# First layer of a four-layer kernel: W products paired over two slots, convolution taps paired in odd slots, and four smaller moves

## The chip, the cores and the metric

The kernel runs on one core of a Trainium2 chip. The metric is the device time in microseconds of one execution. Engines are called PE (matrix engine), ACT (scalar engine), DVE (vector engine), POOL (GpSimd) and SP (the engine that issues most of the DMAs here).

## The reference

Four layers run one after the other on `x` of shape (4, 64, 64, 128), each as `x = x + layer(group_norm(x))`. Only the first layer is touched by the change; the other three (a Fourier layer, a spectral attention layer, a neighbourhood attention layer) stay as they are. The first layer is a two-dimensional selective scan. Cut to what is computed, for each of the 4 images:

```python
xz = gn(x) @ in_proj_w.T                 # 128 -> 512 channels
xh, z = split(xz, 2); z = silu(z)        # 256 channels each
xc = silu(depthwise_conv3x3(xh) + conv_b)
x0 = xc by rows, x1 = xc by columns      # (256, 4096)
xs = [x0, x1, reversed x0, reversed x1]  # 4 directions k
dts, B, C = split(x_proj_weight[k] @ xs[k], [8, 24])      # 8, 16, 16 rows
delta = softplus(dt_projs_weight[k] @ dts + dt_bias[k])   # (256, 4096)
# for each of 16 states n, along the 4096 positions:
h[n] = exp(delta * A[k, :, n]) * h[n] + delta * xs[k] * B[n]
y[k] = sum over n of h[n] * C[n], plus D * xs[k]
y = the four directions put back in place and added
out = (layer_norm(y) * z) @ out_proj_w.T
```

## The kernel before

**Units and slots.** `layer0` walks over 128 units: 4 images, 4 directions k, 8 pieces of 512 positions. A unit has 16 slots, one for each state n, so there are 2,048 slots. In the text, "slot 4" is the slot with n = 4 of some unit. The order in which instructions are written is the order on each engine (a manual schedule); the tile pools put in the waits.

**One slot.** POOL forms `dB` (L684: `du` times a row of B, 128x1024). For each of the two channel halves, ACT computes `dA` into a bank of PSUM (L689, three banks in rotation) and DVE runs the scan into `h` (L690). Then `transposed()` is called. It puts eight transposes of older states on PE (L538, into the single PSUM tile `pt`, two banks), then the W products of the tile transposed one slot before (L573: four matmuls of 32 columns each, `yT <- hT, W`, side by side in the array), and hands back a copy on ACT (L548, `hT <- pt`). "T" below is the eight transposes, "W products" the four matmuls. The transposes run 7 slots behind the scan (`LAG = 7`).

**The two `yT` banks.** The W products accumulate over the four groups of four states. For an earlier unit the last groups' products fall in slots 4 to 7 of the next one: the first of the two `yT` tiles is complete in slot 5, the second in slot 7. Each is then taken out (for the first direction of an image by a copy, L587, else by an add on DVE, L589), and the next unit starts to fill them in slot 8.

**The steps of the next unit.** A table gives them fixed places: in slot 6 on PE the small product `xd_ps` (L448, 48 rows), in slot 7 on ACT two copies out of it (`xd` L451 and `Ct` L456), in slots 7 and 9 on PE the two products `dp` (L465), from slot 8 to 12 the softplus (ACT L468 and L471, DVE L474) and `du` (POOL L477).

**Side work.** The input side of the next image and the output side of the previous one are generators. Each `yield` names a kind of piece, and after each slot at most one piece is put in, if `Side.due` says that the work is behind its pace (pieces done against slots gone by). A convolution has nine taps (L159, matmuls of 128x512 into one PSUM bank `cv`); one may start only in slot 11, and once it has started, `Side.inside` makes every following slot carry one tap, so it runs from slot 11 to slot 3 of the next unit. There are 52 such convolutions. They, and every other small product of the side work and of the steps, use one PSUM bank (`spare`, tag "m").

**Silu.** `silu` uses ACT three times (Exp, Ln, Exp; L631) and DVE once (L358). `later(place, ..., slots=...)` puts each in a given later slot: "act0" is behind the first `dA` of the slot, "act1" behind the second, "act2" behind the copy `hT`, "dve" ahead of the scans. After a convolution, that ends in slot 3, the Exp comes in slot 4 (act0), the Ln in slot 4 (act1), the second Exp in slot 5 (act0), the product on DVE in slot 6, and a copy by columns on ACT (`by_columns`, L369) in slot 7. The gates `z` are computed in the same way: a product `zp` (L177), Exp, Ln and Exp all in the slot after, the product on DVE in the slot after that.

Of the kernel before, what the change touches and what calls it, by code (L numbers as in the profile page):

```python
# [11 lines left out]
F32 = mybir.dt.float32  # L12
# [5 lines left out]
P = 128  # L18
# [64 lines left out]
def layer0(sh, A, x_in, x_out, scr, ahead):  # L83
# [7 lines left out]
    with ExitStack() as ctx:  # L91
# [60 lines left out]
        def conv(xn, s, bank):  # L152

            for t in range(9):
                yield "c"
                if t == 0:
                    pm = bank("cv")
                dy, dx = divmod(t, 3)
                nc.tensor.matmul(  # L159
                    pm,  # L160
                    lhsT=taps[:, s, t, :],
                    rhs=xn[:, dy : dy + 8, dx : dx + 64],
                    start=(t == 0),
                    stop=(t == 8),
                )
            return pm

        def grown(b, c, s, pm, later, e=None, gather=None):
            bias = conv_b[:, s : s + 1], conv_nb[:, s : s + 1]
            xo = silu(pm, *bias, scr(f"xr{b % 2}")[s, :, c * CH : (c + 1) * CH], later, (0, 1, 2), e)  # L170
            later("act0", gather or by_columns, xo, scr(f"xw{b % 2}")[s], c, slots=4)

        def gates(b, c, v, bank, later, es=(None, None)):
            for s in range(2):
                yield "z"
                zp = bank("zp")
                nc.tensor.matmul(zp, lhsT=w_in[:, 2 + s, :], rhs=v, start=True, stop=True)  # L177
                silu(zp, 0.0, 0.0, scr(f"z{b % 3}")[s, :, c * CH : (c + 1) * CH], later, (0, 0, 1), es[s])

        def rows():  # L180
            xn = tmp.tile([P, 10, 66], F32, name="xn", bufs=3)
# [170 lines left out]
        def silu(v, bias, minus, dst, later, wait, e=None):  # L352

            if e is None:
                e = tmp.tile([P, CH], F32, name="e", tag="t2", bufs=4)

            def product():
                nc.vector.scalar_tensor_tensor(e, v, bias, e, ALU.add, ALU.mult)  # L358
                nc.sync.dma_start(dst, e)

            later("act0", nc.scalar.activation, e, v, AF.Exp, scale=-1.0, bias=minus)
            later("act1", nc.scalar.activation, e, e, AF.Ln, bias=1.0, slots=1 + wait[0])
            later("act0" if wait[1] else "act2", nc.scalar.activation, e, e, AF.Exp, scale=-1.0, slots=1 + wait[1])
            later("dve", product, slots=1 + wait[2])
            return e

        def by_columns(xo, dst, c):
# [6 lines left out]
        def after(b, st, later, bands):  # L374

            for c in bands:
                yield "l"
                rows = slice(c * CH, (c + 1) * CH)
                if kept:
                    y = kept.pop()  # L380
                else:
                    y = tmp.tile([P, 4, 2 * P], F32, name="yf", tag="t4", bufs=4)
                    nc.sync.dma_start(y, tiles(scr(f"y2{b % 2}")[rows, :]))
                z = tmp.tile([P, 2, CH], F32, name="zf", tag="t4", bufs=4)
                nc.sync.dma_start(z, scr(f"z{b % 3}")[:, :, rows].rearrange("s p t -> p s t"))
# [12 lines left out]
                yg = tmp.tile([P, 2, CH], F32, name="yg", bufs=2)  # L398
                for s in range(2):
                    yield "m"  # L400
                    pt = spare("pg")
                    for q in range(4):
                        nc.tensor.transpose(pt[:, q * P : (q + 1) * P], y[:, q, s * P : (s + 1) * P], sh.ident)
                    norm = dict(scale=on_w[:, s : s + 1], bias=on_b[:, s : s + 1])
                    later("act0", nc.scalar.activation, yg[:, s, :], pt, AF.Identity, **norm)
                yield "f"
                xr = tmp.tile([P, 4, DM], F32, name="xr", tag="t2", bufs=4)
                nc.sync.dma_start(xr, tiles(x_in(b)[rows, :]))
                if b < NB - 1:
# [28 lines left out]
        def inputs(k, c, u, par, spare):  # L438
# [3 lines left out]
            du = tmp.tile([P, 2, CH], F32, name="du")  # L442
            bank = {}

            def project():
                bank["x"] = spare("xd_ps")[0:48, :]
                for s in range(2):
                    nc.tensor.matmul(bank["x"], lhsT=w_x[:, s, k, :], rhs=u[:, s, :], start=(s == 0), stop=(s == 1))  # L448

# [39 lines left out]
            return Bb  # L489

        spare = lambda name: psm.tile([P, CH], F32, name=name, tag="m")
        ring = [0]

        def any_bank(name):
# [25 lines left out]

        LAG = 7
        queue = []
        copied = None

        def transposed():

            nonlocal copied
            todo, copied = copied, None
            pt = None
            if queue:  # L530
                G = queue[0]
                q = G["q"]
                G["q"] += 1
                pt = ps.tile([P, 4, 2, P], F32, name="pt")
                for j in range(4):
                    t0 = q * P + j * 32
                    for s in range(2):
                        nc.tensor.transpose(  # L538
                            pt[:, j, s, :], G["h"][:, s, t0 : t0 + 32, :].rearrange("p t n -> p (t n)"), sh.ident
                        )  # L540
                if q == 3:
                    queue.pop(0)
            if todo is not None:
                products(*todo)
            if pt is not None:
                hT = tmp.tile([P, 4, 2 * P], F32, name="hT")
                copied = G, q, hT
                return lambda: nc.scalar.copy(hT, pt.rearrange("p j s d -> p j (s d)"))  # L548
            return lambda: None

# [78 lines left out]
        def later(place, f, *a, slots=1, **kw):  # L629

            todo.setdefault((slot + slots, place), []).append(lambda: f(*a, **kw))  # L631
# [10 lines left out]
        with tc.manual_schedule(engines=order):  # L642
            idle = lambda: None
            left = opening(any_bank, [idle, fetched, idle, begun, grown_steps, readied])
            u, ready, bd, Wd, Bb = (got[n] for n in ("u", "ready", "bd", "Wd", "Bb"))
            sides.append(Side(rest(left, spare, later), 18 * len(left), 0, 2 * NS * len(left)))
            for i, (b, k, c) in enumerate(units):
                if i % per == 0:
                    ln_st = small.tile([P, NJ, 1, 6], F32, name="ln_st")
                    first = len(left) if b == 0 else 0  # L650
                    if b + 1 < NB:
                        sides.insert(len(sides) if b == 0 else 0, Side(before(b + 1, spare, later), 17 + 8 * 22, NS * (i + first), (28 - first) * NS))
                rev = k >= 2
                pos = orders[b].index(k)
                pc = NCH - 1 - c if rev else c
# [16 lines left out]
                for n in range(NS):  # L672
# [14 lines left out]
                    for s in range(2):  # L687
# [4 lines left out]
                        )  # L692
                        steps(n, f"act{s}")
                        flush(f"act{s}")
                    copy = transposed() if slot >= LAG else (lambda: None)
                    copy()
                    steps(n, "act2")
                    flush("act2")
# [26 lines left out]

                    inside = [d for d in sides if d.inside]
                    free = not inside and slot >= taken
                    for d in inside or [d for d in sides if free and n in SIDE[d.need] and d.due(slot)][:1]:
                        taken = slot + SPACE[d.need]
                        d.free_at = slot + 1  # L730
                        d.step()
# [40 lines left out]
class Side:  # L772
# [7 lines left out]
    @property  # L780
    def inside(self):

        return self.need == "c" and self.run % 9 > 0

    def due(self, slot):
        wait = self.need == "l" and self.loads and slot < self.loads[0]
# [1404 lines left out]
```

## Time and profile before

| what | value |
|---|---|
| median of 3 runs | 7696.86 us (7693.64 to 7699.71) |
| the profiled execution, its time | 7694.64 us |
| its span, first to last instruction | 7692.9 us |
| mean granted clock of PE | 0.965 |
| first scan starts, last scan ends | 112.8 us, 5645.7 us |
| busy share of the span: PE, DVE, ACT, POOL | 82%, 88%, 79%, 74% |
| busy in 500 to 1500 us: PE, DVE, ACT, POOL | 85%, 98%, 95%, 93% |

The last row is from the busy times of that stretch alone: in the first layer four engines are nearly full at once, and the shares over the whole span mix this with the other three layers. A row of a group reads: line, engine, operation, output and inputs with their shapes, how often; then busy time in all and the mean of one; then the idle time of the engine just before these instructions, and what ended most of it. A row of the timeline reads: start, length, engine, line, operation, tiles, how many in a row, and in brackets the idle time before and what ended it. A matmul of 512 columns shows as two records, as does each W product (so a tap is "x2", and the four W products are "x8"); a transpose is one record.

### The profile page before, as it was taken

What the parts mean: (1) busy time and instruction counts of PE and PEld (TensorE: products, weight loads), DVE (VectorE), ACT (ScalarE), POOL (GpSimd) and SP (SyncE); (2) the same over time, 40 slices, a digit from 0 to 9 for tenths busy, and PEclk for the clock granted to TensorE, in tenths of its full rate; (3) what the DMA queues carried; (4) which work ended last, traced back from release to release, by engine and by line L of the source; (5) the groups of instructions that cost most, each with busy time, mean ns of one, the idle gap of its engine ahead of it and who ended that gap; (6) DMA issues with size and microseconds to landing.
All of it is one profiled execution on the core that took longest, in us unless ns stands there. A gap on an engine that the chain in (4) does not pass through costs nothing.

```text
span 7692.9 us, 140985 instructions
## 1 busy us (share of the span) xinstructions
PE 6324.7 (82%) x52796; PEld 3997.2 (52%) x52796; DVE 6751.7 (88%) x8113; ACT 6094.9 (79%) x9683; POOL 5694.2 (74%) x2718
## 2 busy tenths in 40 slices
PE   7888888888889877888887777787789978676789
PEld 3544444444455544445554444454467756564566
DVE  7999999999999999999999999999966655656678
ACT  7999999999999999999999999999843323314667
POOL 4999999999999999999999999999930024123233
PEclk8999999999999999999999999999999978788899
DMA  6555556555656655465565445555532241231332
GB/s 173 171 169 177 176 171 180 168 172 166 189 174 182 189 188 171 155 183 184 174 193 185 166 168 180 176 182 180 176 107 67 63 115 52 77 103 41 103 97 81
DMA packets 1325856, 1158.87 MB, mean 151 GB/s; under 512 B 694134, under 2 KB 1119698, under 8 KB 1258227
## 3 DMA queue, kind: packets, MB, share of 16 engines
q1 hardware_dynamic: 1320898, 1147.43, 48.7%
q8 instruction: 416, 6.82, 0.4%
q10 hardware_dynamic: 4272, 2.43, 0.1%
q14 instruction: 270, 2.20, 0.1%
HBM read 956.37 MB, written 189.21 MB: 149 GB/s over the span
## 4 chain that ended last, share of the span: by engine, by line
PE 34%; ACT 31%; DVE 19%; issue 8%; POOL 4%; DMA 2%; SPq 1%; ACTq 0%; DVEq 0%; POOLq 0%
ACT hT L548 12%; DVE h L690 12%; ACT dA L689 12%; PE pt L538 7%; PE cv L159 5%; PE yT L573 4%; POOL dB L684 3%; ACT e L631 2%; PE pf L917 2%; PE po L930 1%; ACT delta L468 1%; PE pt L1870 1%; PE pu L1161 1%; PE pa L1161 1%; PE pb L1161 1%
## 5 line engine op out<-in xcount | busy, mean ns | idle before, releaser
L690 DVE TENSOR_TENSOR_SCAN h<-dA,state,dB 128x512 f32<-128x512 f32 x4096 | 4921.4, 1268 | 127.0 <-POOL dB L684 48.0
L684 POOL TENSOR_TENSOR dB<-du,Bb 128x1024 f32<-128x1024 f32 x2048 | 4816.6, 2391 | 162.2 <-DVE h L690 121.9
L538 PE MATMUL pt<-ident,h 128*128 128x128 f32 x16384 | 2221.1, 279 | 824.8 <-ACT hT L548 809.6
L689 ACT ACTIVATE dA<-delta,A_neg 128x512 f32<-128x512 f32 x4096 | 2750.0, 695 | 118.3 <-DVE h L690 95.8
L538 PEld LDWEIGHTS pt<-ident,h 128*128 128x128 f32 x16384 | 1810.0, 142 | 1866.0 <-ACT hT L548 1642.5
L548 ACT COPY hT<-pt 128x1024 f32<-128x1024 f32 x2048 | 2077.2, 1014 | 178.6 <-PE pt L538 158.6
L573 PE MATMUL yT<-hT,W 128*32 128x256 f32 x16384 | 1380.2, 409 | 0.3
L573 PEld LDWEIGHTS yT<-hT,W 128*32 128x32 f32 x16384 | 455.8, 150 | 342.6 <-issue 330.2
L159 PE MATMUL cv<-xn,taps 128*128 128x512 f32 x936 | 526.9, 644 | 2.9 <-DVE delta L474 2.9
L1161 POOL TENSOR_TENSOR xg<-xg,so 128x1024 f32<-128x1024 f32 x16 | 39.3, 2467 | 620.0 <-PE pu L1161 619.4
L1908 POOL TENSOR_TENSOR S<-S,sm 128x784 f32<-128x784 f32 x128 | 191.4, 1495 | 414.6 <-DVE sm L1906 243.1
L477 POOL TENSOR_TENSOR du<-delta,u 128x512 f32<-128x512 f32 x256 | 329.2, 1286 | 188.7 <-DVE delta L474 172.3
L465 PE MATMUL dp<-xd,w_dt 65*128 65x512 f32 x512 | 288.7, 646 | 65.7 <-ACT Ct L456 43.8
L448 PE MATMUL xd_ps<-u,w_x 128*48 128x512 f32 x512 | 249.4, 610 | 18.8 <-DVE e L358 17.6
L1915 ACT ACTIVATE S<-S,mx 128x196 f32<-128x196 f32 x512 | 228.0, 449 | 32.2 <-DVE mx L1942 29.8
L159 PEld LDWEIGHTS cv<-xn,taps 128*128 128x128 f32 x936 | 139.2, 188 | 180.6 <-issue 163.2
L918 ACT ACTIVATE h<-pf,b 128x512 f32<-128x512 f32 x128 | 87.7, 687 | 118.8 <-PE pf L917 100.7
L474 DVE SCALAR_TENSOR_TENSOR delta<-delta,dp 128x512 f32<-128x512 f32 x256 | 171.2, 669 | 3.9 <-ACT delta L471 0.8
L1161 POOL TENSOR_TENSOR WX<-wr,Xs 128x544 f32<-128x544 f32 x40 | 60.7, 1517 | 152.2 <-issue 62.9
L1870 PE MATMUL pt<-ident,S 128*98 128x128 f32 x1024 | 166.3, 287 | 3.4 <-POOL S L1908 2.0
L1161 DVE TENSOR_TENSOR WX<-wr,Xs 128x544 f32<-128x544 f32 x88 | 74.1, 860 | 104.4 <-PE pz L1161 59.5
L465 PEld LDWEIGHTS dp<-xd,w_dt 65*128 65x128 f32 x512 | 76.5, 188 | 170.7 <-ACT Ct L456 97.4
(377 smaller groups left out, 7101.9 us busy)
## 6 DMA issues: line engine op xcount, KB each, us to landing
Bb<-l_B SPq DMA_DIRECT2D x512, 1024.0 KB
W<-l_W SPq DMA_DIRECT2D x512, 256.0 KB
l_y<-y SPq DMA_DIRECT2D x127, 512.0 KB
u<-l_xr SPq DMA_DIRECT2D x64, 512.0 KB
u<-l_xw SPq DMA_DIRECT2D x64, 512.0 KB
y<-l_y SPq DMA_DIRECT2D x56, 512.0 KB
V<-l_v SPq DMA_DIRECT2D x512, 49.0 KB
y<-l_y SPq DMA_DIRECT2D x80, 256.0 KB
```

The source lines that it names most:

```text
L159: nc.tensor.matmul(pm, lhsT=taps[:, s, t, :], rhs=xn[:, dy : dy + 8, dx : dx + 64], start=(t == 0), stop=(t == 8),)
L448: nc.tensor.matmul(bank["x"], lhsT=w_x[:, s, k, :], rhs=u[:, s, :], start=(s == 0), stop=(s == 1))
L465: nc.tensor.matmul(bank[s], lhsT=w_dt[:, k, s * P : (s + 1) * P], rhs=xd, start=True, stop=True)
L477: nc.gpsimd.tensor_tensor(du[:, s, :], delta[:, s, :], u[:, s, :], ALU.mult)
L538: nc.tensor.transpose(pt[:, j, s, :], G["h"][:, s, t0 : t0 + 32, :].rearrange("p t n -> p (t n)"), sh.ident)
L548: return lambda: nc.scalar.copy(hT, pt.rearrange("p j s d -> p j (s d)"))
L573: nc.tensor.matmul(U["yT"][e][32 * jo : 32 * jo + 32, qo % 2, :], lhsT=U["Ws"][G["g"]][:, :, 4 * q + j], rhs=hT[:, j, :], start=((e, jo) n ...
L684: nc.gpsimd.tensor_tensor(dB, du, B_now[:, q : q + 1, :].to_broadcast([P, 2, CH]), ALU.mult)
L689: nc.scalar.activation(dA, delta[:, s, :], AF.Exp, scale=A_neg[:, k, s, n : n + 1])
L690: nc.vector.tensor_tensor_scan(h[:, s, :, q], dA, dB[:, s, :], state[:, s, n : n + 1], ALU.mult, ALU.add)
L1161: r = f(*args, **kw)
L1870: nc.tensor.transpose(pt[:, half, hp, :], U["S"][:, e, hp, 98 * half : 98 * half + 98], sh.ident)
```

## The change

- **W products in pairs.** In slots 1, 3, 11, 13 and 15 `transposed` holds the W products back; the next slot puts in both, one group behind the other. For this `hT` has three buffers in place of two, and `yg` has one in place of two.
- **Taps in pairs.** `conv` yields at every second tap, and a convolution that has started goes on only in odd slots: two taps each in slots 11, 13, 15 and 1, one in slot 3. The counts that set the side work's pace follow (10 for 18, 14 for 22), and `inside` counts 5 pieces for 9.
- **`xd_ps` in a free `yT` bank.** In slot 6 it takes the `yT` tile that was complete in slot 5.
- **Silu spread.** After a convolution: Exp in slot 4, Ln in slot 5, Exp in slot 6 (all act0), product on DVE in slot 7. For `z` the new form gives the places that it had.
- **Column copy** in slot 13 in place of slot 7 (`slots=10`).

```diff
             for t in range(9):
-                yield "c"
+                if t % 2 == 0:
+                    yield "c"
...
         def grown(b, c, s, pm, later, e=None, gather=None):
-            xo = silu(pm, *bias, scr(f"xr{b % 2}")[s, :, c * CH : (c + 1) * CH], later, (0, 1, 2), e)
-            later("act0", gather or by_columns, xo, scr(f"xw{b % 2}")[s], c, slots=4)
+            xo = silu(pm, *bias, scr(f"xr{b % 2}")[s, :, c * CH : (c + 1) * CH], later, (("act0", 2), ("act0", 3), 4), e)
+            later("act0", gather or by_columns, xo, scr(f"xw{b % 2}")[s], c, slots=10)
...
-                silu(zp, ..., later, (0, 0, 1), es[s])
+                silu(zp, ..., later, (("act1", 1), ("act2", 1), 2), es[s])
...
-            later("act1", nc.scalar.activation, e, e, AF.Ln, bias=1.0, slots=1 + wait[0])
-            later("act0" if wait[1] else "act2", nc.scalar.activation, e, e, AF.Exp, scale=-1.0, slots=1 + wait[1])
-            later("dve", product, slots=1 + wait[2])
+            (log, a), (exp, b), c = wait
+            later(log, nc.scalar.activation, e, e, AF.Ln, bias=1.0, slots=a)
+            later(exp, nc.scalar.activation, e, e, AF.Exp, scale=-1.0, slots=b)
+            later("dve", product, slots=c)
...
-                yg = tmp.tile([P, 2, CH], F32, name="yg", bufs=2)
+                yg = tmp.tile([P, 2, CH], F32, name="yg", bufs=1)
...
+            outer = spare if spare is any_bank else free_bank
             def project():
-                bank["x"] = spare("xd_ps")[0:48, :]
+                bank["x"] = outer("xd_ps")[0:48, :]
...
+        free_bank = lambda name: psy.tile([P, 2, 2 * P], F32, name=f"yT{int(first_out)}").rearrange("p r d -> p (r d)")
...
-        copied = None
-        def transposed():
-            nonlocal copied
-            todo, copied = copied, None
+        copied = []
+        def transposed(hold=False):
+            todo, copied[:] = copied[:], []
...
-            if todo is not None:
-                products(*todo)
+            if hold:
+                copied[:] = todo
+            else:
+                for each in todo:
+                    products(*each)
             if pt is not None:
-                hT = tmp.tile([P, 4, 2 * P], F32, name="hT")
-                copied = G, q, hT
+                hT = tmp.tile([P, 4, 2 * P], F32, name="hT", bufs=3)
+                copied.append((G, q, hT))
...
-            sides.append(Side(rest(left, spare, later), 18 * len(left), 0, 2 * NS * len(left)))
+            sides.append(Side(rest(left, spare, later), 10 * len(left), 0, 2 * NS * len(left)))
...
-  Side(before(b + 1, spare, later), 17 + 8 * 22, NS * (i + first), (28 - first) * NS)
+  Side(before(b + 1, spare, later), 17 + 8 * 14, NS * (i + first), (28 - first) * NS)
+                first_out = i > 0 and rev
...
-                    copy = transposed() if slot >= LAG else (lambda: None)
+                    copy = transposed(n in {1, 3, 11, 13, 15}) if slot >= LAG else (lambda: None)
...
-                    for d in inside or [d for d in sides if free and n in SIDE[d.need] and d.due(slot)][:1]:
+                    for d in [d for d in inside if n % 2] or [d for d in sides if free and n in SIDE[d.need] and d.due(slot)][:1]:
...
     def inside(self):
-        return self.need == "c" and self.run % 9 > 0
+        return self.need == "c" and self.run % 5 > 0
```

More of the change, by code (lines that the diff above doesn't have):

```diff
@@ L177, in gates @@
                 nc.tensor.matmul(zp, lhsT=w_in[:, 2 + s, :], rhs=v, start=True, stop=True)
-                silu(zp, 0.0, 0.0, scr(f"z{b % 3}")[s, :, c * CH : (c + 1) * CH], later, (0, 0, 1), es[s])
+                silu(zp, 0.0, 0.0, scr(f"z{b % 3}")[s, :, c * CH : (c + 1) * CH], later, (("act1", 1), ("act2", 1), 2), es[s])
         def rows():
@@ L651, in layer0 @@
                     if b + 1 < NB:
-                        sides.insert(len(sides) if b == 0 else 0, Side(before(b + 1, spare, later), 17 + 8 * 22, NS * (i + first), (28 - first) * NS))
+                        sides.insert(len(sides) if b == 0 else 0, Side(before(b + 1, spare, later), 17 + 8 * 14, NS * (i + first), (28 - first) * NS))
+                first_out = i > 0 and rev
                 rev = k >= 2
```

## The prediction

> **What bounds the kernel now.** I read the page's groups first, then the busy times of three stretches, then the timeline around a convolution.
>
> ```profile
> L690 DVE TENSOR_TENSOR_SCAN h<-dA,state,dB 128x512 f32<-128x512 f32 x4096 | 4921.4, 1268 | 127.0 <-POOL dB L684 48.0
> L684 POOL TENSOR_TENSOR dB<-du,Bb 128x1024 f32<-128x1024 f32 x2048 | 4816.6, 2391 | 162.2 <-DVE h L690 121.9
> L538 PE MATMUL pt<-ident,h 128*128 128x128 f32 x16384 | 2221.1, 279 | 824.8 <-ACT hT L548 809.6
> ```
>
> The scans alone fill 4921 us of the first layer's 5533. Over that stretch DVE is idle 145 us in all, so no rearrangement can win more than that and what hides in lengthened slots. In the starts of the scans a slot with nothing else on DVE lasts 2.35 us; this is the floor.
>
> ```profile
> core 0: us, PE busy (x) PEld busy (x) DVE busy (x) ACT busy (x) POOL busy (x), PEclk, DMA share, GB/s
> 1060.57:1078.27 17.70, 17.70 (x128) 10.18 (x127) 17.42 (x15) 15.52 (x22) 16.66 (x8) 1.00 0.70 242
> 1078.27:1083.90 5.63, 3.33 (x33) 2.10 (x31) 4.75 (x5) 5.63 (x10) 5.41 (x4) 1.00 0.41 130
> 603.00:612.73 9.73, 7.51 (x73) 4.52 (x70) 9.73 (x10) 9.60 (x13) 9.73 (x6) 1.00 0.55 167
> ```
>
> While taps run, PE is full (17.70 of 17.70). Just after, ACT is full (5.63 of 5.63) and DVE is not. Elsewhere (603 us) DVE and POOL are.
>
> ```profile
> 1060.57 1.03 PE L538 MATMUL pt<-ident,h 128*128 128x128 f32 x8
> 1061.53 0.67 PE L573 MATMUL yT<-hT,W 128*32 128x256 f32 x8
> 1062.13 1.13 PE L159 MATMUL cv<-xn,taps 128*128 128x512 f32 x2
> 1063.10 1.04 PE L538 MATMUL pt<-ident,h 128*128 128x128 f32 x8
> ```
>
> A tap slot on PE is T 0.96, W products 0.60, tap 0.97: 2.53 us, 0.18 over the floor. ACT's `dA` runs ahead of the scans by some 0.6 us in slot 12 and has about 0.2 left in slot 0; from slot 15 to 3 the scans follow PE at 2.51 to 2.54. Then comes slot 4:
>
> ```profile
> 1078.46 0.69 ACT L631 ACTIVATE e<-cv,conv_nb 128x512 f32<-128x512 f32 x1
> 1079.05 0.69 ACT L689 ACTIVATE dA<-delta,A_neg 128x512 f32<-128x512 f32 x1
> 1079.66 0.62 ACT L631 ACTIVATE e<-e 128x512 f32<-128x512 f32 x1
> 1080.18 1.00 ACT L548 COPY hT<-pt 128x1024 f32<-128x1024 f32 x1
> 1081.08 0.70 ACT L689 ACTIVATE dA<-delta,A_neg 128x512 f32<-128x512 f32 x1
> ...
> 1081.88 2.46 DVE L690 TENSOR_TENSOR_SCAN h<-dA,state,dB 128x512 f32<-128x512 f32 x2 [0.83 <-ACT dA L689]
> ```
>
> Exp and Ln stand between two `dA`, and the scan waits 0.83 us. Over the 52 convolutions, from the trace: slots 12 to 3 last 19.62 us in the mean where eight floors are 18.84 (40 us in all); DVE's idle time in slot 4 is 0.80 (42 us), in slot 7 it is 0.32 (17 us), where ACT has `xd`, `Ct` and the column copy.
>
> [...] A transpose follows another after 0.109 us, but the 32-column W products follow one after 0.202; the first transpose behind W products takes 0.164; the first half of a tap behind W products 0.534, where a half inside a row of taps takes 0.43. [...] PE's 85% hides stretches where it sets the pace.
>
> **The change part by part** (against the profiled execution, 7694.6 us: span 7692.9 and 1.7 around it; the median is 2.2 above it).
>
> *Pairs on PE.* Odd slot: T 0.164 + 6 x 0.109 = 0.82; step to the tap 0.11 if it costs what a transpose to another full-width product (`D_diag`) shows, up to 0.53 if it stalls as behind W products; four halves at 0.43 = 1.72. Sum 2.65. Even slot: T 0.76 + 0.20, then two groups of W products; one is 0.27 + 0.02 + 0.31 with its exit, two are some 0.27 more for each half, 1.15. Sum 2.11. The pair takes 4.76 (5.2 at the dear end) for 5.05 before, 4.71 at the floor. Saved are one entry (0.09), one exit and re-entry (0.04 + 0.055) and 0.105 on one tap, 0.29 in all. In place of 0.18 per slot, PE loses 0.03. The pair is uneven, though: `hT` copies come 2.65 and 2.11 apart, so ACT's lead must cover about 0.3 at the worst phase. ACT's own cycle without extras is 2.14 (two `dA` 1.20, copy 0.94), so it keeps up in the short half. I keep 12 of the 40 us and count 28 saved; nothing saved at the dear end, all 40 at the best.
>
> Where no convolution runs, the hold delays W products by a slot. Nothing reads them before slot 5, which is not held; PE idles there anyway (T waits for the copy, 810 us in all). The third `hT` buffer is what lets the copy go on. Zero.
>
> *Silu spread.* Slot 4 loses the Ln: 0.53 on ACT's chain. ACT then needs 2.67 there against 2.35, with a lead that pairs have left some tenths larger. I take 0.2 idle for 0.80: 0.6 x 52 = 31 us (22 if the lead stays as it is, 42 at most). Slot 5 has the Ln where it had the Exp; slot 6 the Exp, 0.53, behind 0.66 us of DVE's add, with a lead of over 1 us: hidden. The product moves from slot 6 to 7. Queued behind it in the bank is `dp`, which has to wait for `xd` anyway (0.23 in the timeline), at about the same moment: zero.
>
> *Column copy.* Slot 7 loses 1.06 us of ACT and keeps 0.53 of the moved Exp: of 0.32 idle I take 0.2 back, 10 us. In slot 13 it meets two cases. With taps running (some 26 times) it delays one `hT` copy by about 0.5, which takes lead; this is in the 12 us kept. Beside a gate (14 units in the order of the built program):
>
> ```profile
> 1103.12 0.70 ACT L689 ACTIVATE dA<-delta,A_neg 128x512 f32<-128x512 f32 x1
> ...
> 1104.48 0.60 ACT L631 ACTIVATE e<-zp 128x512 f32<-128x512 f32 x1 [0.66 <-PE zp L177]
> ```
>
> It stands ahead of this Exp, and ACT waits 0.66 to 1.05 us there for `zp`. The copy fills that wait and overruns it by up to 0.4: 14 x 0.3 = 4 us lost; 15 if the cover is gone.
>
> *`xd_ps` in a `yT` bank.* It leaves the small bank, which after a convolution it had to wait for (silu's product). New is the wait for the add:
>
> ```profile
> 612.15 0.66 DVE L589 TENSOR_TENSOR y<-y,yT 128x512 f32<-128x512 f32 x1
> 612.42 1.92 PE L448 MATMUL xd_ps<-u,w_x 128*48 128x512 f32 x4
> ```
>
> Here it started 0.39 before the add ended; in 49 of the 128 units it did so, by 0.1 to 1.4, 0.57 in the mean. Queued behind it on PE are T of slot 7, the copy `hT`, the next `dA`. But `xd` also waits for slot 7's second `dA` (614.04), and that for the first scan after the add, so 0.4 of delay on PE is some 0.1 on ACT, inside a lead of 0.5 to 0.8. Zero; 28 us (49 x 0.57) if all of it shows. `dp` no longer waits for `Ct`; uncounted.
>
> *Order.* The second `zp` stands behind two W groups where it was behind one: 14 x 0.15 = 2 us. `yg` has uses far apart: zero. The side work keeps its 52 convolutions and ends units before the image does: zero. POOL sets nothing new: `dB` leads by 0.3 to 0.5 us in slots 13 to 0, at 2.345 per slot.
>
> Sum: -28 - 31 - 10 + 4 + 2 = -63 us. 7694.6 - 63 = 7632; with the median's 2.2, 7634.
>
> **Rivals.**
>
> *A. Half of it* (POOL or the uneven pair takes over). `dB`'s lead of 0.3 in slot 13 is the smallest in the loop, and POOL's 2.39 per `dB` is longer than the floor if overlap is lost. With DVE held at 2.39 through eight slots and slot 4 at 0.4 idle: 14 + 21 saved, less 6, 7668. Against it: that lead grew in every slot up to the 4th.
>
> *B. Slower: the odd slot is too long.* The step from transposes to taps costs 0.53, and the second W group costs a full 0.60: pairs of 5.25. Then 52 convolutions with 4.5 pairs each lose 0.54 over the floor, 126 us for 40, and 41 come back in slots 4 and 7: +45, 7742. The point from which it decides is a pair of some 5.06. For it: the trace has no step from transposes to taps. Against: transposes to `D_diag` at 0.109 have the same width.
>
> *C. No change.* The leads swallow what is saved: slot 4's stall moves to slots 5 and 6, where the Exp now is, and PE's pair ends near 5.0. 7694 to 7700. Against it: lead in slot 6 is 1.1 to 1.7.
>
> *D. All of it*: 40 + 42 + 17 less nothing, 7598.
>
> **Numbers.** The forecast (7610 to 7655) has 0.55, A 0.17, D and beyond 0.08, C 0.08, B and the borrowed bank's wait 0.12. A difference under 0.2% (15 us) can't be told from none. From these cases: faster 0.80, same 0.08, slower 0.12. The range 7588 to 7700 leaves out B and a few in a hundred below.
>
> **What would show it.** In the profile after: tap pairs as "x4" behind "x8" transposes in odd slots and W products "x16" in even ones, T to T near 2.65 and 2.1; DVE without the 0.83 idle after a convolution; slots 15 to 3 near 2.38; `xd_ps` with waits on `y` or `DVE`, and T of slot 7 a little later. Wrong: a pair over 5.0, idle on DVE in slots 5, 6 or 14, `dp` waiting for the product (L358), or `dB` named as what ends the scans' waits.

## The result, and the profile after

The changed kernel takes 7675.83 us, the median of six runs (7661.97 to 7688.09), against 7696.13 us (7689.61 to 7700.2) for the kernel before, measured beside it. The ratio is 0.9973, with a 95% interval of 0.9963 to 0.9983. The forecast was 7634: the sign is right and the value lies in the range, but of the 62 us forecast only 20 came.

The profiled execution took 7663.36 us, with a span of 7661.4. From the start of the first scan to the end of the last it needs 5506.0 us, where the kernel before needed 5532.9. So 27 of its 31 us are won in the first layer, where the change was made. The rest is spread over what lies outside, which the change leaves alone.

The groups of the changed kernel (busy time and mean of one; then idle time before, and what ended most of it):

```profile
L698 DVE TENSOR_TENSOR_SCAN h<-dA,state,dB 128x512 f32<-128x512 f32 x4096 | 4923.7, 1269 | 96.4 <-ACT dA L697 50.7
L692 POOL TENSOR_TENSOR dB<-du,Bb 128x1024 f32<-128x1024 f32 x2048 | 4813.4, 2387 | 162.2 <-DVE h L698 137.9
L542 PE MATMUL pt<-ident,h 128*128 128x128 f32 x16384 | 2239.1, 280 | 911.5 <-ACT hT L555 843.1
```

The scans wait 96.4 us where they waited 127.0; the work itself has not changed. What ends most of the wait is now ACT's `dA`, where it was POOL's `dB`. The transposes wait 87 us longer than before. That is the first sign of what went wrong, and it can't be read as a loss by itself, since PE is not the bound everywhere.

The timeline of PE while taps run, changed kernel:

```profile
545.04 1.09 PE L542 MATMUL pt<-ident,h 128*128 128x128 f32 x8
545.97 1.88 PE L160 MATMUL cv<-xn,taps 128*128 128x512 f32 x4
547.69 1.04 PE L542 MATMUL pt<-ident,h 128*128 128x128 f32 x8
548.65 1.11 PE L580 MATMUL yT<-hT,W 128*32 128x256 f32 x16
549.89 1.09 PE L542 MATMUL pt<-ident,h 128*128 128x128 f32 x8
```

This is the pair as forecast: transposes and two taps, then transposes and two groups of W products. The starts of the transposes stand 2.65 and 2.20 us apart, 4.85 for the pair. Before, two slots took 5.05.

The busy times of two stretches of the changed kernel, the end of a convolution and the slots just after it:

```profile
core 0: us, PE busy (x) PEld busy (x) DVE busy (x) ACT busy (x) POOL busy (x), PEclk, DMA share, GB/s
505.66:515.40 9.74, 9.18 (x74) 5.79 (x73) 9.66 (x9) 8.90 (x13) 9.74 (x5) 1.00 0.46 155
515.40:520.31 4.91, 3.48 (x39) 2.14 (x37) 4.77 (x5) 4.91 (x9) 4.91 (x3) 1.00 1.05 283
```

In the first, PE is no longer full (9.18 of 9.74). In the second, ACT still is (4.91 of 4.91), but now DVE nearly is too (4.77, where it had 4.75 of 5.63). The timeline of ACT and DVE there:

```profile
512.15 8.73 DVE L698 TENSOR_TENSOR_SCAN h<-dA,state,dB 128x512 f32<-128x512 f32 x7
515.53 0.68 ACT L638 ACTIVATE e<-cv,conv_nb 128x512 f32<-128x512 f32 x1
516.10 0.69 ACT L697 ACTIVATE dA<-delta,A_neg 128x512 f32<-128x512 f32 x1
516.72 1.01 ACT L555 COPY hT<-pt 128x1024 f32<-128x1024 f32 x1
517.63 0.69 ACT L697 ACTIVATE dA<-delta,A_neg 128x512 f32<-128x512 f32 x1
518.25 0.62 ACT L638 ACTIVATE e<-e 128x512 f32<-128x512 f32 x1
```

The 0.83 us wait of the kernel before is gone: seven scans run through, with Exp and Ln in different slots. Two of the three main steps are thus in the trace as they were forecast.

**Where the rest went.** I took the length of each of the 2,048 slots from the starts of the scans. Summed over all 128 units, and as differences to the kernel before, this tells in which slots the time was won or lost (us, one profiled execution each; the other kernels are those of the experiments below). What DVE runs ahead of a slot's first scan counts in the slot before it, so silu's product has gone from the fifth to the sixth, both in one column here.

| kernel | slots 0 to 3 | 4 to 6 | 7 and 8 | 9 to 12 | 13 | 14 and 15 | sum |
|---|---|---|---|---|---|---|---|
| the change | -17 | -26 | -29 | -2 | +28 | +20 | -27 |
| e3_hold_with_taps | -20 | -31 | -28 | -2 | +27 | +5 | -49 |
| e4_taps_split | -14 | -31 | -28 | -1 | +2 | +15 | -58 |
| f1_no_pairs | +2 | -18 | -30 | -2 | +13 | 0 | -36 |
| f2_pairs_alone | -5 | -3 | -6 | +14 | +5 | +15 | +21 |
| f3_fill | -3 | -21 | -33 | -2 | +27 | +11 | -20 |
| f4_silu_together | -16 | -9 | -26 | -2 | +1 | +15 | -38 |
| g2_no_pairs_split | +1 | -21 | -31 | -1 | 0 | +7 | -44 |

The change won 74 us in slots 0 to 12 and lost 47 in slots 13 to 15. Some 8 us on both sides are only side work in another place: in slot 14 DVE has 10 us more work of its own than before, in slots 0 and 4 together 8 less. Without these the gains are 66 us, where the forecast had 69 (28, 31 and 10), and the losses 39, where it had 6. Two things in the trace stood out in slots 13 to 15.

*Slot 13.* The timeline of the changed kernel in a slot 13 with taps running:

```profile
538.61 1.02 ACT L555 COPY hT<-pt 128x1024 f32<-128x1024 f32 x1 [0.44 <-PE pt L542]
539.52 0.70 ACT L697 ACTIVATE dA<-delta,A_neg 128x512 f32<-128x512 f32 x1
540.14 1.16 ACT L371 COPY xw<-e 128x512 f32<-128x512 f32 x1
541.06 0.72 ACT L697 ACTIVATE dA<-delta,A_neg 128x512 f32<-128x512 f32 x1
541.69 1.03 ACT L555 COPY hT<-pt 128x1024 f32<-128x1024 f32 x1
541.81 1.29 DVE L698 TENSOR_TENSOR_SCAN h<-dA,state,dB 128x512 f32<-128x512 f32 x1 [0.21 <-ACT dA L697]
542.77 1.09 PE L542 MATMUL pt<-ident,h 128*128 128x128 f32 x8 [0.28 <-ACT hT L555]
543.41 4.81 DVE L698 TENSOR_TENSOR_SCAN h<-dA,state,dB 128x512 f32<-128x512 f32 x4 [0.30 <-ACT dA L697]
```

The `hT` copy waits 0.44 for PE's transposes, which come late behind the two taps of slot 11. After that ACT would have to catch up. Instead the column copy (1.16 us) stands between the two `dA`, the next `hT` copy starts 3.08 us after the last one, and both DVE (0.21 and 0.30) and PE (0.28) wait. In the 30 units in which an earlier convolution's column copy meets running taps, slot 13 takes 3.10 us for 2.37: 22 us.

*PE's clock.* The mean granted clock fell from 0.965 to 0.961. Of the stretches at half clock that begin between the first and the last scan, the trace before has 13, 58 us together; the trace after has 33, 123 us together (some last two or three times 3.41 us). Busy times of two stretches of the changed kernel, just after a convolution's unit, with a gate:

```profile
core 0: us, PE busy (x) PEld busy (x) DVE busy (x) ACT busy (x) POOL busy (x), PEclk, DMA share, GB/s
709.90:713.31 3.41, 1.57 (x20) 1.29 (x24) 3.41 (x5) 3.41 (x6) 3.41 (x3) 0.99 1.15 272
713.31:716.72 3.41, 3.41 (x17) 1.46 (x10) 3.22 (x3) 1.98 (x4) 3.29 (x2) 0.51 1.83 48
```

and the timeline there:

```profile
708.73 1.03 PE L542 MATMUL pt<-ident,h 128*128 128x128 f32 x8
711.74 1.09 PE L542 MATMUL pt<-ident,h 128*128 128x128 f32 x8 [1.97 <-ACT hT L555]
712.76 1.56 PE L580 MATMUL yT<-hT,W 128*32 128x256 f32 x16
714.26 2.08 PE L178 MATMUL zp<-xn,w_in 128*128 128x512 f32 x2
716.13 1.31 PE L542 MATMUL pt<-ident,h 128*128 128x128 f32 x8
716.37 0.60 ACT L638 ACTIVATE e<-zp 128x512 f32<-128x512 f32 x1 [1.43 <-PE zp L178]
717.58 1.28 DVE L698 TENSOR_TENSOR_SCAN h<-dA,state,dB 128x512 f32<-128x512 f32 x1 [1.05 <-ACT dA L697]
```

No tap runs here, so a held slot (its transposes start at 708.73) leaves PE with the transposes alone, and then PE waits 1.97 us. In the first stretch PE works 1.57 of 3.41 us. In the next it is granted half its clock (0.51) and is full: the gate's product `zp` takes 2.08 us, ACT waits 1.43 for it, and the scan 1.05. In all 33 stretches the 3.4 us ahead had PE busy for 0.11 to 0.50 of the time; before, for 0.08 to 0.51. So ahead of each of them PE was idle for about half of that time or more, and in no case was it without work for all of it.

So there were two theories for the experiments. **P**: the column copy in slot 13 falls into the short half of a pair and costs 22 to 30 us. **H**: holding W products where no tap runs empties PE, the clock is halved more often, and that costs about 20 us. Rivals: **R1**, the uneven pair costs by itself; **R2**, the clock is chance and has nothing to do with the hold.

### The profile page after: what moved, and what is told of

Read it like the earlier page. It is cut to its first block, busy times and chain, and to the rows that moved or that the text cites. A ratio compares the mean times of both kernels' runs of the same rounds, so it can differ in the third digit from the quotient of the medians.

```text
span 7661.4 us, 140502 instructions
## 1 busy us (share of the span) xinstructions
PE 6204.6 (81%) x52796; PEld 4066.9 (53%) x52796; DVE 6742.4 (88%) x8113; ACT 6082.2 (79%) x9683; POOL 5688.3 (74%) x2718
## 4 chain that ended last, share of the span: by engine, by line
ACT 34%; PE 31%; DVE 22%; issue 8%; POOL 3%; DMA 2%; SPq 1%; ACTq 0%; DVEq 0%; POOLq 0%
ACT hT L555 14%; DVE h L698 14%; ACT dA L697 13%; PE pt L542 6%; PE cv L160 4%; POOL dB L692 2%; ACT e L638 2%; PE pf L925 2%; PE pz L1169 1%; PE po L938 1%; PE yT L580 1%; PE pu L1169 1%; PE pt L1878 1%; DVE delta L478 1%; PE pa L1169 1%
## 5 line engine op out<-in xcount | busy, mean ns | idle before, releaser
L698 DVE TENSOR_TENSOR_SCAN h<-dA,state,dB 128x512 f32<-128x512 f32 x4096 | 4923.7, 1269 | 96.4 <-ACT dA L697 50.7
L580 PE MATMUL yT<-hT,W 128*32 128x256 f32 x16384 | 1243.5, 405 | 0.4
L580 PEld LDWEIGHTS yT<-hT,W 128*32 128x32 f32 x16384 | 517.8, 148 | 316.9 <-issue 237.6
L160 PE MATMUL cv<-xn,taps 128*128 128x512 f32 x936 | 449.8, 598 | 21.0 <-DVE delta L478 20.8
L452 PE MATMUL yT<-u,w_x 128*48 128x512 f32 x508 | 245.1, 605 | 21.1 <-DVE y L596 20.8
L160 PEld LDWEIGHTS cv<-xn,taps 128*128 128x128 f32 x936 | 156.8, 190 | 132.9 <-issue 108.7
L475 ACT ACTIVATE delta<-delta 128x512 f32<-128x512 f32 x256 | 164.6, 643 | 0.0
L472 ACT ACTIVATE delta<-dp 128x512 f32<-128x512 f32 x256 | 152.3, 595 | 12.3 <-PE dp L469 11.9
```

The costliest lines, as they stand in the source:

```text
L160: nc.tensor.matmul(pm, lhsT=taps[:, s, t, :], rhs=xn[:, dy : dy + 8, dx : dx + 64], start=(t == 0), stop=(t == 8),)
L580: nc.tensor.matmul(U["yT"][e][32 * jo : 32 * jo + 32, qo % 2, :], lhsT=U["Ws"][G["g"]][:, :, 4 * q + j], rhs=hT[:, j, :], start=((e, jo) n ...
L698: nc.vector.tensor_tensor_scan(h[:, s, :, q], dA, dB[:, s, :], state[:, s, n : n + 1], ALU.mult, ALU.add)
```

## The experiments

Each changed kernel has five runs (the change itself six, e1_col7 four, f3_fill ten, f2_pairs_alone fifteen); "ratio" is to the kernel before, beside which each was run, with its 95% interval. Stretches at half clock are those that begin between first and last scan of the profiled execution.

| kernel | median us (range) | ratio | stretches | scans, us |
|---|---|---|---|---|
| before | 7696.13 (7689.61 to 7700.2) | | 13 | 5532.9 |
| the change | 7675.83 (7661.97 to 7688.09) | 0.9973 (0.9963 to 0.9983) | 33 | 5506.0 |
| e1_col7 | 7763.4 (7758.35 to 7769.97) | 1.0093 (1.0077 to 1.0108) | 55 | 5601.8 |
| e2_col12 | 7656.76 (7646.02 to 7672.21) | 0.9953 (0.9941 to 0.9966) | 36 | 5507.3 |
| e3_hold_with_taps | 7646.56 (7639.59 to 7648.83) | 0.9935 (0.9923 to 0.9948) | 10 | 5483.6 |
| e4_taps_split | 7632.78 (7630.48 to 7637.78) | 0.9921 (0.9909 to 0.9933) | 13 | 5475.4 |
| f1_no_pairs | 7657.6 (7652.5 to 7663.52) | 0.9954 (0.9942 to 0.9967) | 8 | 5496.8 |
| f2_pairs_alone | 7705.54 (7699.55 to 7718.74) | 1.0016 (1.0009 to 1.0024) | 43 | 5553.5 |
| f3_fill | 7678.21 (7667.6 to 7684.36) | 0.9976 (0.9967 to 0.9986) | 5 | 5512.6 |
| f4_silu_together | 7657.72 (7650.73 to 7667.18) | 0.9954 (0.9941 to 0.9966) | 11 | 5494.8 |
| g1_small_bank | 7654.39 (7650.6 to 7657.87) | 0.9946 (0.9933 to 0.996) | 11 | 5494.0 |
| g2_no_pairs_split | 7657.62 (7647.3 to 7660.69) | 0.9949 (0.9936 to 0.9961) | 7 | 5489.0 |
| g3_col9 | 7652.81 (7649.95 to 7663.56) | 0.9948 (0.9935 to 0.996) | 13 | 5494.5 |

The last column is the time from first to last scan in the one profiled execution. It leaves out the later layers, which are the same in all these kernels and still took from 2039.8 to 2055.3 us in the profiled executions. Where two medians are a few microseconds apart, this column says how much of it the first layer can have. A profiled execution need not be a middle one: that of the change is the second fastest of six, that of e2_col12 the slowest of five. The kernel before has medians of 7693.0, 7695.8 and 7694.5 us beside the e, f and g kernels and 7696.1 beside the change, so a difference of medians between these groups can be off by some 3 us.

### Where the column copy stands

e1_col7 puts the column copy back into slot 7, e2_col12 into slot 12; all else is as in the change.

```
-  later("act0", gather or by_columns, xo, ..., c, slots=10)
+  later("act0", gather or by_columns, xo, ..., c, slots=4)    # e1_col7
+  later("act0", gather or by_columns, xo, ..., c, slots=9)    # e2_col12
```

> The changed kernel, the column copy alone back in slot 7. Theory P (the copy in slot 13 falls into the short half of a pair, where ACT has no room): slot 13 with taps goes from 3.09 us back to 2.37 to 2.45, 30 x 0.7 = 21 us saved, 4 more beside the gates; slot 7 takes back 0.2 to 0.35 x 52 = 10 to 18 us. In all 7661 to 7671 us against 7676 for the changed kernel. Rival R1 (the uneven pair itself makes slot 13 long, the copy is innocent): slot 13 stays near 3 us and slot 7 gets dearer, 7686 to 7694 us.

> The changed kernel, the column copy in slot 12, the long half of the pair, where ACT waits 0.44 us for PE in the trace. Theory P: slots 12 and 13 together lose 0.3 where they lost 0.72 over the floor, 7662 to 7670 us. Rival R1: the place of the copy is of no matter, 7676 us within 6.

The median of e2_col12 is 19 us below the change's. In the 30 units slot 13 is back at 2.37 us and slot 12 lengthens from 2.38 to 2.69: 9 us lost for 22. P holds in the slots. The profiled execution, the slowest of the five, has no shorter scan part, so the 19 us are not to be put down to the slots alone.

e1_col7 missed its expectation by far, and for another reason. The change had also moved silu's product on DVE from slot 6 to slot 7, and the copy reads what that product writes. What the copies `xw` of e1_col7 waited for:

```profile
its engine sat idle before it (us, times) until:
  DVE e L359: 53.2, 52
```

ACT stood still for 1.0 us in each of 52 convolutions, slot 7 went from 3.14 to 4.59 us, and the stretches at half clock to 55. So its time is no price for slot 13. The slot itself, though, is at 2.37 us in the 30 units, with the pairs in place and the copy gone, where R1 expected it near 3. The run also says that in the changed kernel the column copy can't go back alone: its move and the silu spread belong together.

### Where the hold stands

e3_hold_with_taps holds W products only in a slot that carries taps.

```
-  copy = transposed(n in {1, 3, 11, 13, 15}) if slot >= LAG else ...
+  chosen = [d for d in sides if d.inside] or [d for d in sides if slot >= taken and n in SIDE[d.need] and d.due(slot)][:1]
+  hold = n in {1, 3, 11, 13, 15} and any(d.need == "c" for d in chosen)
+  copy = transposed(hold) if slot >= LAG else ...
```

> The changed kernel, but W products are held back only in slots that carry taps, not in every odd slot. Theory H (holding without taps leaves PE so idle that the clock is granted at half for 3.4 us at a time): stretches at half clock between the first and the last scan go from 33 to 12 to 18, each worth about 1 us: 7654 to 7662 us, and the runs lie within 12 us of each other where they were 26 apart. Rival R2 (those stretches come by chance, or from the taps): some 33 again, 7676 us within 6, the same scatter.

It is 29 us faster than the change, more than expected; the intervals of the two ratios lie apart. The timeline of PE at the same place as in the last fence, e3_hold_with_taps:

```profile
710.70 1.09 PE L542 MATMUL pt<-ident,h 128*128 128x128 f32 x8 [1.37 <-ACT hT L555]
711.72 0.67 PE L580 MATMUL yT<-hT,W 128*32 128x256 f32 x8
712.32 1.13 PE L178 MATMUL zp<-xn,w_in 128*128 128x512 f32 x2
713.36 1.09 PE L542 MATMUL pt<-ident,h 128*128 128x128 f32 x8
```

With one group of W products in every slot, `zp` takes 1.13 us, where under half clock it took 2.08. The stretches fall from 33 to 10. In the units that follow a convolution and have none themselves, slots 14 and 15 together take 15 us less over the 22 units. The runs also scatter less, 9 us from fastest to slowest where the change has 26.

f3_fill goes the other way: it keeps every hold of the change and gives PE work instead. In held slots without taps, four of the eight transposes are done twice into the same place.

```
-  for j in range(4):
+  for j in [*range(again), *range(4)]:     # again = 2 in held slots without taps
```

> The changed kernel with useless work added: in odd slots without taps PE does four of the eight transposes twice, into the same place, some 380 x 0.44 = 165 us of PE time. Theory H (half clock follows idleness of PE, not the holding as such): stretches at half clock fall from 33 to below 22, and in spite of more work the time falls to 7655 to 7668 us. Rival (more work on PE can only delay the copies): 7680 us or more.

The timeline of PE, f3_fill, near the same unit:

```profile
712.53 1.09 PE L542 MATMUL pt<-ident,h 128*128 128x128 f32 x8 [1.55 <-ACT hT L555]
713.55 1.10 PE L580 MATMUL yT<-hT,W 128*32 128x256 f32 x16
714.58 1.13 PE L178 MATMUL zp<-xn,w_in 128*128 128x512 f32 x2
715.55 1.47 PE L542 MATMUL pt<-ident,h 128*128 128x128 f32 x12
```

The held slots have twelve transposes now ("x12"; 1,512 more in all), and with them the stretches fall from 33 to 5, the clock rises to 0.969, and `zp` is back at 1.13 us although W products are still held. So the count of stretches follows PE's activity, not the order of W products. The time was missed: 7678, no faster than the change. Slots 14 and 15 won 9 us and slots 0 to 6 lost 20; there the added transposes stand in front of the `hT` copy, which I take for the reason. Hence its time gives no price for the stretches. The slots do. The change, f3_fill and e3_hold_with_taps put nearly all their work into the same slots, so they can be compared slot by slot. Take the slots that in the change touch a stretch at half clock, or follow such a slot, and do not in the other kernel. In 102 of these f3_fill, which still holds, wins 20 us, and what it loses lies elsewhere. In 86 of these e3_hold_with_taps wins 18 of its 22 us; its 1,914 slots that stand beside no stretch in either kernel win 6. So the half clock itself costs 18 to 20 us, somewhat under 1 us a stretch, and little is left for the hold as such. R2 falls: kernels that hold outside taps have 33, 36, 43 and 55 stretches, those that don't have 7 to 13, and the one with filler 5. The mean granted clock says the same of every run: 0.954 to 0.962 in the 30 runs of the first four, 0.965 to 0.969 in the 45 of the others here.

### Both mended

e4_taps_split is e3_hold_with_taps with the column copy in two halves, in slots 12 and 14, where a pair leaves ACT more room.

```
-  later("act0", by_columns, xo, ..., c, slots=10)
+  later("act0", half_columns, xo, xw, 0, ..., slots=9)     # rows 0 to 3
+  later("act0", half_columns, xo, xw, 1, ..., slots=11)    # rows 4 to 7, then the DMA
```

> W products held back only with taps, and the column copy cut into two halves of four image rows, in slots 12 and 14, the long halves of two pairs. Theories P and H together: slot 13 with taps near 2.4, slots 12 and 14 within 0.15 of the floor, and few stretches at half clock: 7638 to 7650 us. R1 and R2: 7670 to 7680 us.

This is the fastest kernel: 7632.78 us, 0.9921 of the time before and 43 us faster than the change. The timeline of ACT and DVE, e4_taps_split, in slots 12 to 14 of such a unit:

```profile
532.58 24.13 DVE L712 TENSOR_TENSOR_SCAN h<-dA,state,dB 128x512 f32<-128x512 f32 x20
533.84 0.71 ACT L711 ACTIVATE dA<-delta,A_neg 128x512 f32<-128x512 f32 x1
534.46 0.68 ACT L384 COPY xw<-e 128x256 f32<-128x256 f32 x1
534.91 0.71 ACT L711 ACTIVATE dA<-delta,A_neg 128x512 f32<-128x512 f32 x1
539.40 0.67 ACT L384 COPY xw<-e 128x256 f32<-128x256 f32 x1
```

Twenty scans run through without a wait, past both halves. Slots 12, 13 and 14 of the 30 units take 2.39, 2.37 and 2.49 us. Over all units slot 13 wins 26 us on e3_hold_with_taps and slots 12, 14, 15 and 0 give 14 back; the medians differ by 14, the scan parts by 8.

g3_col9 is e3_hold_with_taps with the whole copy in slot 9 (`slots=6`), to see whether any slot without taps would do.

> Held only with taps, the whole column copy in slot 9, where no convolution runs and DVE has one product more to do than in slot 8. Theory P (the copy costs what ACT's lead can't cover: 0.6 to 1.1 us of lead in slot 9): slots 9 to 11 lose 0.2 to 0.4 per convolution, 10 to 20 us where slot 13 lost 30: 7633 to 7645 us. Rival: the copy costs its 1.06 us wherever it stands, 7660 us or more.

It would not: 7652.81. Slots 9 and 10 lose 34 us where slot 13 wins 27. In that part of the unit ACT has the softplus, and slots 8 and 10 take 2.99 and 2.93 us already.

### The parts one by one

f1_no_pairs is the change without any pairing: a tap in each slot, no hold, the counts as before.

```
-  if t % 2 == 0:
-      yield "c"
+  yield "c"
-  copy = transposed(n in {1, 3, 11, 13, 15}) ...
+  copy = transposed() ...
```

> The changed kernel with the pairs undone (one tap and one slot's W products per slot, as before); silu spread, borrowed bank and column copy in slot 13 stay. Theory (the prediction's parts, plus P and H): slots 15 to 3 stay at 2.5 us, slot 4 keeps about half of its stall (0.4), slot 13 with taps is 0.6 over because PE leaves ACT only 0.3 per slot there, and half clock is as rare as before (13 stretches): 7670 to 7685 us. Rival (the pairs bring nothing, the other parts all): 7650 to 7660 us.

f2_pairs_alone is the kernel before with only the pairing of taps and W products.

> The kernel before with the pairs alone (taps and W products, held in every odd slot as in the change). Theory: slots 15 to 3 fall to 2.4 (20 us saved), slot 4 keeps some 0.5 of its 0.8 us (15 saved), 30 or more stretches at half clock take 20 us back: 7670 to 7685 us. Rival (without the spread silu the pairs' lead is of no use): slot 4 keeps 0.8, 7690 to 7700 us.

Both miss what was expected: f1_no_pairs lies in its rival's range, f2_pairs_alone above both of its ranges. As it was made, the pairing is a loss. Without it the change is 18 us faster (9 in the scan part; the profiled execution of the change is one of its fastest), and alone on the kernel before it costs 9.7 us (1.0016, interval above one). There, slot 4 after a convolution gains only from 3.29 to 3.10 us, because Exp and Ln still stand together, and the stretches at half clock are 43, 178 us.

g2_no_pairs_split is f1_no_pairs with the column copy in halves: the same as e4_taps_split without pairs.

> Pairs undone, all else as in the best (silu spread, borrowed bank, column copy in halves in slots 12 and 14). If pairs, freed of half clock and of the copy in their short half, save PE time in slots 15 to 3 (20 us) and in slot 4 (10 us): 7650 to 7662 us against 7633. Rival (they are worth nothing even then): 7630 to 7638 us.

7657.62 against 7632.78, 25 us by the medians and 14 by the scan parts: once nothing is held without taps and no whole copy falls into slot 13, the pairs pay. R1 falls as the cause of the loss. The slot table shows what they do: slots 0 to 3 win 15 us and slots 4 to 6 another 10, since ACT comes out of the taps with more lead; slots 14 and 15 give 8 back. That last part stays in every kernel with pairs. It is the side work named above: with single taps DVE has no more work in slot 14 than before; with pairs, whose pace puts the pieces into other slots, it has 10 us more, and 8 less in slots 0 and 4. Without pairs the halves change no median (7657.62 against 7657.6), though slot 13 gives 12 us back to them: over all units a whole copy in slot 13 costs 12 us with single taps and 26 with pairs. In the units with taps alone it costs 0.27 us with single taps (2.64 for 2.37) and 0.73 with pairs (3.10 for 2.37).

f4_silu_together is e4_taps_split with Exp and Ln of the convolution's silu in one slot again.

```
-  later, (("act0", 2), ("act0", 3), 4), e)
+  later, (("act1", 1), ("act0", 2), 3), e)
```

> The best so far (held only with taps, column copy in halves in slots 12 and 14) with the silu as before: Exp and Ln in slot 4, Exp in slot 5, product in slot 6. The prediction's step on the silu: slot 4 gets 0.4 to 0.5 us longer, 52 times, 20 to 28 us: 7653 to 7662 us against 7633. Rival (the lead left by the pairs is enough to cover both): 7631 to 7638 us.

The silu spread is worth 25 us by the medians and 19 by the scan parts. Slots 4, 5 and 6 after a convolution take 2.60, 3.21 and 3.01 us with it (8.82) and 3.12, 3.76 and 2.37 without (9.25): 22 us over the 52.

g1_small_bank is f4_silu_together with `xd_ps` in the small bank again (`outer = spare`).

> The kernel with the silu as before (held only with taps, column copy in halves), now with xd_ps back in the small bank: the borrowed bank alone undone, against 7658 us. Prediction's step: the bank is worth nothing either way, 7655 to 7662 us. Rival G1 (the wait for the small bank after a convolution fed slot 7's stall): slot 7 longer by 0.1 to 0.2 after a convolution and dp waits for Ct again, 7663 to 7672 us. Rival G2 (the wait for the add on the borrowed bank costs): 7640 to 7652 us.

7654.39 against 7657.72, and 5494.0 against 5494.8 in the scan part: the borrowed bank brings nothing and costs nothing that can be measured. This holds with the silu's product in slot 6. With the product in slot 7, as in the change, `xd_ps` of slot 6 would have to wait for it in the small bank; no run has that.

## Why the prediction was right or wrong

By its own terms, with the slot table: forecast were -28 for the pairs, -31 for the silu, -10 for slot 7, +4 and +2 for gates, -63 in all. Measured in the change are -17 in slots 0 to 3, -26 in slots 4 to 6, -29 in slots 7 and 8, -2 in slots 9 to 12, +28 in slot 13 and +20 in slots 14 and 15: -27 in the profiled execution, which is one of the faster ones. The gains came, in sum about as forecast once the moved side work is set aside (66 of 69); two losses came that the sum had at zero or in an allowance.

*Pairs on PE: right in the mechanism, short in the worth.* The pair takes 4.85 us for 4.76 forecast. The unknown step from transposes to taps was the cheap one, 0.109 us, and the taps' halves 0.43. What was too small is the two groups of W products: 1.24 us to the next transposes where 1.15 was forecast. With both failed steps mended, the pairs give 14 us (scan parts) to 25 (medians) for 28 (e4_taps_split against g2_no_pairs_split); with the hold alone mended, 13 and 11 (e3_hold_with_taps against f1_no_pairs). Rival B needed a pair of 5.06, and falls.

*"Where no convolution runs, the hold delays W products by a slot … Zero": failed.* I asked who reads the W products, and rightly answered that nobody does for a while. I did not ask what PE is left with. In the trace after, a held slot with eight transposes and a wait of 1.97 us left PE busy for 1.57 of 3.41 us, and the `zp` and the transposes of the next 3.41 us ran at a granted 0.51. The hold there cost 22 us by the scan parts and 29 by the medians (e3_hold_with_taps); 18 of the 22 lie at the stretches themselves. PE "idles there anyway" was in my own text, as a reason for calling it free; that idleness was the reason why it was not.

*"With taps running it delays one `hT` copy by about 0.5 … in the 12 us kept": failed.* The place of the copy was right and its price was not. It comes when ACT has just waited for late transposes in the long half of a pair and must catch up in the short half. It costs 0.73 us in each of 30 units, 22 us, where about 0.5 in 26 was to lie inside an allowance of 12 that the pairs needed for themselves. In e2_col12 and e4_taps_split this goes away. Most of it needs the pair: beside single taps the copy costs 0.27 us a unit (f1_no_pairs against g2_no_pairs_split). The gate case, forecast at +4, came about so: in the 22 units that follow a convolution and carry no taps, 14 of them with a gate, slot 13 takes 2.88 us in the change and 2.73 in e4_taps_split, 3 us in all.

*Silu spread: right, a little smaller.* Slot 4 gave 40 us for the 31 forecast, part of it by the pairs' lead, but slots 5 and 6 took 14 back. The forecast called the Ln in slot 5 an even exchange for the Exp and the Exp in slot 6 hidden. Measured by f4_silu_together, the spread is worth 19 to 25 us.

*Column copy out of slot 7: more than forecast.* Slot 7 alone gave 22 us for 10, and slot 8 another 6. How much of this is the copy's is not shown: in f2_pairs_alone, with the copy in its old place, slot 7 already wins 6, and the move was not run by itself.

*`xd_ps` in a free `yT` bank: right as far as it was run.* Zero (g1_small_bank, with the product in slot 6), although PE does wait for the add, as the list of waits of the changed kernel has it, from 500 to 5400 us (us in total, times, the longest):

```profile
PE yT L452 <- DVE y L596: 20.0, 38, 1.3
```

That is 20.0 us in 38 waits. That ACT's lead covers them, as the forecast has it, fits the equal times and was not isolated.

*Rivals and signs.* A, at 7668, is near in size but not in cause: POOL did not take over (from 500 to 5400 us the scans waited 27.0 us for `dB` before and 13.5 after), and the uneven pair only where the copy met it. C fails with the slot table, and D with the two failed steps. Of the signs that would show the forecast wrong, two came, longer idle times of DVE in slots 5 (19 us in all for 7) and 14 (21 for 16). None of them named slot 13 or PE's clock.

The kernel with both failed steps mended takes 7632.8 us, where 7634 was forecast. The two steps together are 43 us. That it comes so close is partly luck: the surplus of slots 7 and 8 pays for what silu and pairs fell short of.

## What to carry to other kernels

Work that is only delayed on an engine with time to spare still changes how that engine's time is spread. Here PE was granted half its clock behind 3.41 us in which it was 0.11 to 0.50 busy (33 times in the trace after), and with other work in the gaps there were 5 such stretches (f3_fill). So ask what is left on the engine over such a time, and batch only where other work fills the gap. When two slots are paired, one becomes long and one short, and another engine must catch up in the short one: put no extra work there, or halve it and put it in the slots with room. Price such a step where it stands in the schedule, not in an allowance that another step already uses.

## What the runs showed of the hardware

- In the trace after, PE was granted half its clock (0.5) in 33 stretches of the first layer, 31 of 3.41 us, one of twice and one of three times that. In the 3.41 us ahead of each it was 0.11 to 0.50 busy, with a longest pause of 0.9 to 2.7 us; in the trace before, with 13 stretches, 0.08 to 0.51 busy, with a longest pause of 1.5 to 3.2 us. Such a gap was not always followed by half the clock: from 3049.30 to 3052.71 us in the trace after PE was busy for 0.71 of 3.41 us, and the clock there and in the 3.41 us behind it was 1.00. What decides stayed open; the busy times are the profile's own, in which the ends of matmuls are modelled.
- The mean granted clock differs from run to run, and with it the time. The change's six runs go from 7662.0 us at 0.962 to 7688.1 at 0.958; e3_hold_with_taps and e4_taps_split, with few such stretches in their profiled executions, scatter by 9 and 7 us.
- Going from transposes to 512-column taps of full width takes 0.109 us, as from one transpose to the next, where going from transposes to the 32-column W products takes 0.202. The step from transposes to the full-width `D_diag` products takes 0.109 too, and from these to the W products 0.205. What is paid for in the step to the W products was not shown.
- A column copy of 128x256 took 0.67 us on ACT where one of 128x512 took 1.16, so halving it costs some 0.2 us of ACT time per convolution (2 x 0.67 less 1.16), and it was still worth it.
